# Layer 0's routed experts in two sets of sorted tokens, with the engines' orders written out; in layer 1's tail, weight loads issued by GpSimd and a flag without a memset

## The chip, the cores and the metric

The kernel runs on one core of a Trainium2 chip. A core has five engines with an instruction stream each: TensorE (PE in the profile, its weight loads PEld), VectorE (DVE), ScalarE (ACT), GpSimd (POOL) and SyncE (SP); an engine executes its stream in order and waits on semaphores for the others. DMAs are issued by SP, ACT or POOL and run on 16 DMA engines. The metric is the device time of one execution in microseconds (us), the median over runs. All arithmetic here is in float32.

## The reference

Two transformer layers with adaptive layer norm over 8 sequences of 256 tokens, width 128: 2048 tokens. Cut to what matters:

```python
mod = (_silu(L0_c) @ L0_wmod).reshape(8, 6, 1, -1)          # sa, ca, ga, sb, cb, gb per sequence
h = _layernorm(x) * (1 + ca) + sa
x = x + ga * _L0_attn_ref(h, ...)                            # 16 heads of 8, causal
h = _layernorm(x) * (1 + cb) + sb
x = x + gb * _L0_ffn_ref(h, ...)

# _L0_ffn_ref: 8 experts, hidden width 512, top 2
shared = new_gelu(xf @ Wfc_s + bfc_s) @ Wproj_s + bproj_s
probs = jax.nn.softmax(xf @ Wr, axis=-1)
topk_p, topk_i = jax.lax.top_k(probs, 2)
topk_p = topk_p / jnp.sum(topk_p, axis=-1, keepdims=True)
gate = gate.at[jnp.arange(N)[:, None], topk_i].add(topk_p)
for e in range(8):
    h = new_gelu(xf @ Wfc[e] + bfc[e]) @ Wproj[e] + bproj[e]
    routed = routed + h * gate[:, e:e + 1]

# layer 1: the same frame; 16 heads of 64, causal; its feed-forward:
router = jax.nn.sigmoid(x @ gate_w + gate_b)                 # 16 experts, width 64, top 2, normalised
all_outputs = einsum(silu(hg) * hu, experts_wd)
return x + _mlp(x, shared_wg, shared_wu, shared_wd) + expert_weighted
```

The two gates of a token in layer 0 are a softmax over the two best logits, since the rest of the softmax cancels when they are divided by their sum.

## The kernel before, in words

Tokens stay in SBUF as `x`, in 4 windows (`NW`) of 512 tokens (`TW`), each of 4 token tiles (`TT`) of 128. `h` holds the transposed, modulated layer norm of a window. Two batches (sequences) make one window. The framework's scheduler orders each engine's instructions by itself, except inside `tc.manual_schedule()`, where the order of the source is the order on every engine; before the change that covers only layer 1's tail.

*Attention of layer 0.* `pipelined` runs 24 units (8 batches, 3 units each): `scores0` computes scores, exponentials (ACT) and causal selects (POOL, line 789); `values0` multiplies by the values two units later, and at a batch's end takes the reciprocal (line 1148) and `finish0` projects (line 1161) and adds to `x`. `also0(n)` runs beside each unit: it pops one step from a list, `st0["steps"]`, into which the layer norm of the next feed-forward window (`layernorm_steps`, parts `normalise` and `modulate`) and `route0` are put when a window's two batches are done. So windows 0 to 2 are normalised and routed inside the attention, window 3 after it.

*Sorting.* `Sorted` moves the tokens of a layer's routed experts into DRAM (`xs`), sorted by expert. Each expert has a region of `cap` rows, all tokens that could come to it. `place` computes the rank of a token in its expert by a matmul of ones with the selection masks, writes row indices (`idx`, line 886), and issues eight indirect scatters for a window from POOL (line 889: 4 tiles, 2 choices). `apart` declares that the scatters of one object don't depend on each other; the last of them stands for all, and every read of `xs` waits for it. `tables`, after the last window, works out some 30 small arrays on DVE: which 128 rows each further tile reads (`rowi`), of which expert (`widx`), and the rows at which each token's two results will lie (`yidx`). An expert's first 128 tokens are a tile of their own; the rest, in tiles of 128, are at most `nd` further tiles. For 2048 tokens with 2 choices each there are 31 of them: 8 + 31 = 39 expert tiles.

*Layer 0's experts* (scheduler's order, lines 1189 to 1295). `wst` are the packed weights of the eight experts (514 KB each; five loaded early, three as the attention's buffers go, line 1194). `shared_hidden(w)` and `shared_project(w)` compute the shared expert for a window; the second also adds the routed experts' output bias by the gates (line 1217), multiplies by `gb` on DVE, and adds to `x` on POOL (line 1221). Then each of 39 tiles: `fetch` (SP load `xg`, for further tiles a POOL indirect load `wt` of an expert's weights, line 994), `turn_tile` (PE transpose, line 1249), `hidden` (4 matmuls, each of two passes, line 1259, and 4 gelus on ACT, line 1261), `project` (line 1270, copied on DVE and stored to `ys` by SP, lines 1274 and 1275). `fetch` runs three tiles ahead, with 4 buffers for `xg`, 5 for `wt`.

*Beginning of layer 1.* `gather(b)` brings the two results of each token of a batch back, with 4 indirect loads from POOL (line 1002), and `combine(b)` weighs and adds them to `x` (lines 1402 to 1406, DVE). Four gathers and `after0(0)` (two combines, then `normalise` and `modulate` of window 0: lines 732 to 753) stand ahead of `project1(0, part)` (line 1416), the first work of layer 1's attention. The other windows follow inside it through `also1`, which pops two steps per unit: gathers of batches 4 to 7, and `after0(1)`, `after0(2)`, `after0(3)`.

*Layer 1's tail* (written order). Windows 0 to 2 of the routed experts run sorted (`z1`), in 10 blocks `m` of four tiles: `turn1`, `hidden1`, `project_tiles` (lines 1587, 1597, 1611). Blocks 0 to 3 use resident weights, 4 and 5 are loaded earlier by SP; `fetch_weights1(m)` loads those of blocks 6 to 9, four transfers of 128 KB each. Here ACT reads the expert's number into a register and issues a plain DMA (line 1648). `tables(ps, rows)` writes `widx` as an expert's first row; with `rows` true it writes one row number per partition, which an indirect load needs. In between, the last window is normalised and routed step by step (`route1_steps`); it is then computed densely (`ffn1_hidden`, `ffn1_project`), while `gather1` and `combine1` bring back the results of the sorted blocks, 24 indirect loads. `flag` checks the reciprocals of all softmaxes (line 1728) for a general path that is not taken here.

Buffers: `ps_a`, `ps_b`, `ps_c` are PSUM tiles with 3, 2 and 3 buffers.

Of the kernel before, what the change touches and what calls it, by code (L numbers as in the profile page):

```python
# [9 lines left out]
F32 = mybir.dt.float32  # L10
# [3 lines left out]
ALU = mybir.AluOpType  # L14
# [19 lines left out]
WF, WB, WPK = FC * P, 2 * FC * P, 2 * FC * P + FC  # L34
R_MIN, R_MAX = 1e-30, 1e20
# [522 lines left out]
def fast_path(ctx: ExitStack, tc: tile.TileContext, i: dict, out: bass.AP, bad: bass.AP):  # L558
# [244 lines left out]
    def top2(*args):  # L803
        for step in top2_steps(*args):
            pass

    def top2_steps(pool, p, s12, best, tag):
# [7 lines left out]
        for k in range(2):  # L815
# [6 lines left out]
            if k == 0:  # L822

                nc.vector.scalar_tensor_tensor(work, s12[:, :, 0, :], -4.0, p, ALU.mult, ALU.add)
                yield
# [6 lines left out]
    class Sorted:  # L832
# [29 lines left out]
        def place(self, n, tokens, ps_):  # L862
# [24 lines left out]
            for j in range(nt):  # L887
                for k in range(2):
                    self.apart(nc.gpsimd.indirect_dma_start(  # L889
                        out=self.xs[:, :], out_offset=bass.IndirectOffsetOnAxis(ap=idx[:, j, k : k + 1], axis=0),  # L890
                        in_=tokens[:, j, :], in_offset=None,
                    ).ins)
# [122 lines left out]
    z0 = Sorted(xp, "0", E0, NW, TT, (2 * NT - 2) // P)  # L1015
    z1 = Sorted(xp, "1", E1, 3, TT, ND1)
    z0.clear(zero)
# [15 lines left out]
    def route0(w, ps_):  # L1033
# [7 lines left out]
        red = r0p.tile([P, TT, 1], F32, tag="red", bufs=2, name=f"red0_{w}")  # L1041
        nc.vector.tensor_reduce(red, lg, AX.X, ALU.max)
        nc.vector.tensor_tensor(p, lg, red.to_broadcast(shape), ALU.subtract)
        nc.scalar.activation(p, p, AF.Exp)
        nc.vector.tensor_reduce(red, p, AX.X, ALU.add)
        nc.vector.reciprocal(red, red)
        nc.vector.tensor_tensor(p, p, red.to_broadcast(shape), ALU.mult)
        s = z0.s12[:, t4]
        g = g12[:, t4]
        top2(r0p, p, s, g, f"0_{w}")  # L1050
        z0.place(w, tokens0[w], ps_)
        pick = r0p.tile([P, TT, 2, E0], F32, tag="pickg", bufs=2, name=f"pickg0_{w}")

        nc.vector.tensor_tensor(red, g[:, :, 0:1], g[:, :, 1:2], ALU.add)
        nc.vector.reciprocal(red, red)
        nc.vector.tensor_tensor(g, g, red.to_broadcast([P, TT, 2]), ALU.mult)
# [3 lines left out]
    with (  # L1060
# [108 lines left out]
        def also0(n):  # L1169
            b, u = divmod(n, 3)  # L1170
            if st0["steps"]:
                st0["steps"].pop(0)()
# [4 lines left out]
            if u == 2 and b:  # L1177
                finish0(b - 1)
                if b % 2 == 0:
                    w = b // 2 - 1  # L1180
                    st0["steps"] += layernorm_steps(w, md[0], SB, CB, f"0b{w}", ps_ln, make_tokens0)
                    st0["steps"].append(lambda w=w: route0(w, ps_ln))

        project0(0)
        pipelined([(b, u) for b in range(B) for u in range(3)], scores0, values0, 2, also0)
        finish0(B - 1)

# [3 lines left out]
    with tc.tile_pool(name="ff0", bufs=2) as fp0:  # L1191
# [31 lines left out]
        last = layernorm_steps(NW - 1, md[0], SB, CB, f"0b{NW - 1}", ps_b, make_tokens0)  # L1223
        last[0]()
        hs = shared_hidden(0)
        last[1]()
        route0(NW - 1, ps_b)
        shared_project(0, hs)

        z0.tables(ps_b, True)  # L1230

# [3 lines left out]
        def fetch(n):  # L1235
            xg = fp0.tile([P, P], F32, tag="xg", bufs=4, name=f"xg_{n}")
            if n < E0:
                nc.sync.dma_start(out=xg, in_=z0.xs[bass.ds(n * z0.cap, P), :])
                wt = wst[n]
            else:  # L1240
                z0.load_rows(xg, n - E0)
                wt = fp0.tile([P, WPK], F32, tag="wt", bufs=5, name=f"wt_{n}")
                z0.load_weights(wt, i["wpk"], n - E0)
            st["x", n] = xg, wt

        def turn_tile(n):
            xg, wt = st["x", n]
            xT_ps = ps_b([P, P], f"xT_{n}")
            nc.tensor.transpose(xT_ps, xg, ident)  # L1249
            xT = fp0.tile([P, P], F32, tag="xT", bufs=3, name=f"xTs_{n}")  # L1250
            nc.vector.tensor_copy(xT, xT_ps)
            st["xT", n] = xT

        def hidden(n):
            xT, wt = st.pop(("xT", n)), st["x", n][1]
            hp = ps_a([P, FC, P], f"hp_{n}")
            hs = fp0.tile([P, FC, P], F32, tag="hst", bufs=3, name=f"hst_{n}")
# [6 lines left out]
            st["hs", n] = hs  # L1264

        def project(n):
            hs, wt = st.pop(("hs", n)), st.pop(("x", n))[1]
            y = ps_c([P, P], f"yt_{n}")
# [4 lines left out]
            ysb = fp0.tile([P, P], F32, tag="ysb", bufs=3, name=f"ysb_{n}")  # L1273
            nc.vector.tensor_copy(ysb, y)  # L1274
            nc.sync.dma_start(out=z0.ys[bass.ts(n, P), :], in_=ysb)

        for n in range(3):
            fetch(n)
        for w in range(1, NW):
            hs = shared_hidden(w)  # L1280
            shared_project(w, hs)
        NTI = E0 + z0.nd
        turn_tile(0)
        for n in range(NTI + 1):
            if n + 3 < NTI:
                fetch(n + 3)
            if n + 1 < NTI:
                turn_tile(n + 1)
            if n < NTI:
                hidden(n)  # L1290
            if n:
                project(n - 1)
# [20 lines left out]
    def route1_steps(w, ps_):  # L1313
# [17 lines left out]
        yield from top2_steps(r1p, p, s, g, f"1_{w}")  # L1331
# [38 lines left out]
    with (  # L1370
# [16 lines left out]
        st1 = {"steps": []}  # L1387

        def gather(b):

            yg = ap1.tile([P, 2, 2, P], F32, tag="yg", bufs=2, name=f"yg_{b}")
            for j in range(2):
                z0.gather(yg[:, j], 2 * b + j)
            st1["yg", b] = yg

        def combine(b):

            yg = st1.pop(("yg", b))
            t = ap1.tile([P, 2, P], F32, tag="t", name=f"tc_{b}")
# [492 lines left out]
```

## Time and profile before

| what | value |
|---|---|
| median of 3 runs | 689.07 us (688.54 to 689.54) |
| the profiled execution | 690.99 us |
| its span in the trace | 688.7 us (2.3 us lie around it) |
| mean granted TensorE clock | 0.929 |
| PE busy | 571.4 us (83%) |
| POOL busy | 308.8 us (45%) |
| DVE busy | 331.0 us (48%) |
| ACT busy | 252.8 us (37%) |
| layer 0's attention: last output matmul ends | 150.7 us |
| first and last tile of the routed experts of layer 0 | 193.2 and 271.3 us |
| layer 1's first projection | 298.3 us |
| last gathers of layer 1 | 650.4 to 680.3 us |

All times of instructions count from the start of the span. In timeline lines the columns are: start, busy time, engine, source line, operation, output<-inputs, shape, count, and in brackets the idle time of the engine before it with what ended it. A queue of an engine (SPq, ACTq, POOLq) issues DMAs. The page also cuts the span in 40 slices with the busy share in tenths. Busy shares average over stages with different limits, so each stage has to be read by itself.

### The profile page before, as it was taken

How to read it: one execution, taken by the hardware profiler on the slowest of the kernel's cores; microseconds unless marked ns; L12 is line 12 of the kernel's file. 1: busy time of each engine (PE TensorE's matmuls, PEld its weight loads, DVE VectorE, ACT ScalarE, POOL GpSimd, SP SyncE). 2: the span in 40 equal slices, each digit the busy share in tenths (PEclk: the TensorE clock that was granted, in tenths of full speed). 3: DMA queues.
4: the chain of work that ended last, by engine and by line, in shares of the span. 5: the costliest groups of instructions: out<-in, count | busy, mean ns of one | idle time of the engine just before them, and what ended most of it. 6: DMA issues, size and time to landing. Idle time of an engine off the chain costs nothing.

```text
span 688.7 us, 12844 instructions
## 1 busy us (share of the span) xinstructions
PE 571.4 (83%) x4899; PEld 404.7 (59%) x4899; DVE 331.0 (48%) x985; ACT 252.8 (37%) x447; POOL 308.8 (45%) x458
## 2 busy tenths in 40 slices
PE   3899878878999997078999998999899958658890
PEld 3455444445799997045667765776576636546460
DVE  5367747674522222374243565254524471534573
ACT  2446343526345555014342363234323521142130
POOL 6576584854713442774121146314631462020173
PEclk9999998999999999569999999999999988977996
DMA  8999940012466995120020203020303043443722
GB/s 288 317 407 400 373 173 9 25 45 83 133 229 207 320 338 176 50 53 21 1 63 1 63 2 81 12 64 1 81 13 63 1 125 101 121 120 92 160 69 81
DMA packets 51712, 85.41 MB, mean 124 GB/s; under 512 B 6332, under 2 KB 29916, under 8 KB 50492
## 3 DMA queue, kind: packets, MB, share of 16 engines
q1 hardware_dynamic: 40940, 57.64, 26.6%
q0 software_dynamic: 8400, 24.78, 11.2%
q10 hardware_dynamic: 2304, 2.10, 1.0%
q8 instruction: 40, 0.66, 0.4%
q14 instruction: 28, 0.23, 0.1%
HBM read 53.43 MB, written 31.07 MB: 123 GB/s over the span
## 4 chain that ended last, share of the span: by engine, by line
PE 36%; DVE 6%; DMA 6%; POOL 5%; issue 3%; ACT 2%; ACTq 1%; SPq 0%; DVEq 0%; POOLq 0%
PE o L1461 5%; PE sc L1441 5%; PE y L1512 4%; PE qp L1416 4%; PE vp L1424 4%; PE kp L1416 4%; POOL yg L1002 3%; PE sum L1469 3%; DMA yg<-ys,yidx 3%; DMA rb<-rd 2%; PE gu L1597 1%; DVE r L1476 1%; POOL xs L889 1%; PE yq L1611 1%; DMA wt<-in_wpk_dram 1%
## 5 line engine op out<-in xcount | busy, mean ns | idle before, releaser
L789 POOL TENSOR_SCALAR_AFFINE_SELECT pt<-pt 128x256 f32<-128x256 f32 (+1 forms) x176 | 89.7, 540 | 152.9 <-ACT pt L1444 133.8
L1444 ACT ACTIVATE pt<-sc 128x768 f32<-128x768 f32 x64 | 48.9, 808 | 87.1 <-PE sc L1441 87.0
L1002 POOL DMA_INDIRECT yg<-ys,yidx x56 | 53.4, 953 | 56.1 <-ACT a L1679 39.6
L889 POOL DMA_INDIRECT xs<-ht,idx x56 | 60.9, 1087 | 23.9 <-issue 14.5
L1117 ACT ACTIVATE pt<-sc 128x1024 f32<-128x1024 f32 x48 | 46.8, 1021 | 53.7 <-PE sc L1113 52.7
L1461 PE MATMUL o<-pt,v 128*64 128x128 f32 (+1 forms) x512 | 53.5, 343 | 5.3 <-POOL pt L789 5.3
L1441 PE MATMUL sc<-q,k 64*128 64x256 f32 (+1 forms) x512 | 55.5, 343 | 0.0
L1441 PEld LDWEIGHTS sc<-q,k 64*128 64x128 f32 x512 | 43.6, 190 | 16.1 <-issue 11.5
L1461 PEld LDWEIGHTS o<-pt,v 128*64 128x64 f32 x512 | 34.2, 141 | 31.1 <-issue 11.4
L994 POOL DMA_INDIRECT wt<-in_wpk_dram,widx x31 | 29.2, 941 | 46.4 <-PE xT L1249 45.0
L593 DVE COPY k<-kp 128x512 f32<-128x512 f32 x29 | 20.1, 692 | 53.7 <-PE kp L1416 53.7
L1261 ACT ACTIVATE hst<-hp,wt 128x128 f32<-128x128 f32 x124 | 35.4, 368 | 26.6 <-ACT hst L1261 17.6
L1113 PE MATMUL sc<-qm,k 32*128 32x512 f32 x192 | 35.9, 681 | 5.0 <-POOL qm L1088 4.4
L1416 PE MATMUL kp<-h,wk 128*128 128x256 f32 x128 | 36.6, 412 | 1.9 <-DVE v L593 1.9
L1416 PE MATMUL qp<-h,wq 128*128 128x256 f32 x128 | 37.6, 413 | 0.6 <-DVE h L753 0.6
L1424 PE MATMUL vp<-wv,h 128*128 128x512 f32 x64 | 37.8, 675 | 0.0
L1274 DVE COPY ysb<-yt 128x128 f32<-128x128 f32 x39 | 11.4, 292 | 54.7 <-PE yt L1270 48.8
L595 ACT COPY v<-vp 128x512 f32<-128x512 f32 x29 | 17.0, 585 | 53.3 <-PE vp L1424 42.6
L593 DVE COPY ou<-o 128x512 f32<-128x512 f32 x29 | 19.9, 687 | 32.1 <-PE o L1461 32.0
L1259 PE MATMUL hp<-xTs,wt 128*128 128x128 f32 x248 | 33.5, 278 | 1.5 <-DMA wt<-in_wpk_dram,widx 0.6
L1270 PE MATMUL yt<-wt,hst 128*128 128x128 f32 x248 | 32.6, 275 | 0.0
L1512 PEld LDWEIGHTS y<-wo,ou 128*128 128x128 f32 x256 | 29.6, 194 | 3.9 <-issue 2.6
(284 smaller groups left out, 1121.4 us busy)
## 6 DMA issues: line engine op xcount, KB each, us to landing
xs<-zero SPq DMA_DIRECT2D x1, 12288.0 KB
xs<-zero SPq DMA_DIRECT2D x1, 8192.0 KB
rb<-rd SPq DMA_DIRECT2D x14, 512.0 KB
wst<-in_wpk_dram SPq DMA_DIRECT2D x8, 514.0 KB
mdb<-mrd SPq DMA_DIRECT2D x2, 2048.0 KB
xg<-xs SPq DMA_DIRECT2D x63, 64.0 KB
ys<-ysb SPq DMA_DIRECT2D x10, 256.0 KB
ys<-ysb SPq DMA_DIRECT2D x39, 64.0 KB
```

The lines of the kernel that those rows point to most:

```text
L593: nc.vector.tensor_copy(dst, src)
L789: nc.gpsimd.affine_select(out=pt, in_=pt, compare_op=ALU.is_ge, fill=0.0, base=0, pattern=[[0, pt.shape[1]], [1, P]], channel_multiplier=-1,)
L889: self.apart(nc.gpsimd.indirect_dma_start(out=self.xs[:, :], out_offset=bass.IndirectOffsetOnAxis(ap=idx[:, j, k : k + 1], axis=0), in_=to ...
L1002: nc.gpsimd.indirect_dma_start(out=yg[:, k, :], out_offset=None, in_=self.ys[:, :], in_offset=bass.IndirectOffsetOnAxis(ap=self.yidx[:, j, ...
L1113: nc.tensor.matmul(out=sc[:, n, :].rearrange("p (a q) -> p a q", q=rhs.shape[2]), lhsT=k[r, cols], rhs=rhs, start=True, stop=True,)
L1117: nc.scalar.activation(pt[:, bass.ts(half, 2), :], sc, AF.Exp)
L1416: nc.tensor.matmul(out=ps_[:, n, :], lhsT=w1[f"w{what}1"][:, bass.ts(2 * part + n, P)], rhs=hb, start=True, stop=True,)
L1424: nc.tensor.matmul(out=vp, lhsT=hb[:, bass.ts(j, P)], rhs=w1["wv1"][:, bass.ts(k, 512)], start=True, stop=True)
L1441: nc.tensor.matmul(out=sc[:, n, cols], lhsT=k[r, c % 2, bass.ts(kb, P)], rhs=q[r, c % 2, qs], start=True, stop=True)
L1444: nc.scalar.activation(pt, sc[:, :, 0:384], AF.Exp, scale=1.0 / math.sqrt(D1))
L1461: nc.tensor.matmul(out=o[bass.ts(n, D1), m, qs], lhsT=v[:, kb, bass.ts(4 * u + 2 * m + n, D1)], rhs=pts[m][:, n, cols], start=(kb == 0), s ...
L1512: nc.tensor.matmul(out=y[:, j, :], lhsT=aT[:, c % 2, c // 2, bass.ts(j, P)], rhs=w1["wo1"][:, c, :], start=(c == 0), stop=(c == NC1 - 1),)
```

## The change

*Two sets.* `z0` becomes `zs0`: one `Sorted` for windows 0 to 2 (23 further tiles, 31 in all) and one for window 3 (7 further tiles, 15 in all), with tables of their own. The tables of the first set are a step of the attention's list.

*Routing of layer 0* becomes a generator with a `yield` between steps. It drops the softmax: the two best are chosen from copied logits, and the gates come from the difference of the two, by one exponential. `also0` pops two steps per unit.

*Written order* now begins before the expert stage and ends after `project1(0, ...)`. Only window 0 of the shared expert stands ahead of the tiles; windows 1 to 3 come after them. In the loop over 46 tiles each iteration takes one step of a chain: first the rest of window 3 (layer norm, logits, choice, placing with one scatter per iteration, gates, tables), later, once the first set is done, gathers and combines of batches 0 to 3 and the layer norm of layer 1's window 0. `fetch` runs four ahead. The layer norm of layer 1's window 1 stands between the shared windows.

*Layer 1's beginning.* Gathers of batches 0 to 3 and `after0(0)`, `after0(1)` are gone from there; `also1` still gathers batches 4 to 7 and runs `after0(2)` and `after0(3)`.

*Tail.* `fetch_weights1` uses `load_weights`, indirect loads from POOL, with row tables; the flag uses a column of an existing array in place of a memset tile, and its matmul comes one step later.

```diff
-    z0 = Sorted(xp, "0", E0, NW, TT, (2 * NT - 2) // P)
+    zs0 = [Sorted(xp, f"0{n}", E0, k, TT, (2 * k * TW - 2) // P) for n, k in enumerate((NW - 1, 1))]
...
-        nc.vector.tensor_reduce(red, lg, AX.X, ALU.max)
-        nc.vector.tensor_tensor(p, lg, red.to_broadcast(shape), ALU.subtract)
-        nc.scalar.activation(p, p, AF.Exp)
-        nc.vector.tensor_reduce(red, p, AX.X, ALU.add)
-        nc.vector.reciprocal(red, red)
-        nc.vector.tensor_tensor(p, p, red.to_broadcast(shape), ALU.mult)
-        s = z0.s12[:, t4]
+        nc.vector.tensor_copy(p, lg)
+        yield
+        z, n = (zs0[0], w) if w < NW - 1 else (zs0[1], 0)
+        s = z.s12[:, bass.ts(n, TT)]
+        best = r0p.tile([P, TT, 2], F32, tag="best", bufs=2, name=f"best0_{w}")
+        yield from top2_steps(r0p, p, s, best, f"0_{w}", LOW)
+        yield
+        yield from z.place_steps(n, tokens0[w], ps_)
+        yield
...
+        nc.vector.tensor_tensor(d, best[:, :, 1:2], best[:, :, 0:1], ALU.subtract)
+        nc.scalar.activation(d, d, AF.Exp)
+        nc.vector.tensor_scalar(g[:, :, 0:1], d, 1.0, None, ALU.add)
+        nc.vector.reciprocal(g[:, :, 0:1], g[:, :, 0:1])
+        nc.vector.tensor_tensor(g[:, :, 1:2], g[:, :, 0:1], d, ALU.mult)
...
-            if st0["steps"]:
-                st0["steps"].pop(0)()
+            for step in st0["steps"][:2]:
+                step()
+            del st0["steps"][:2]
...
+                    if w == NW - 2:
+                        st0["steps"].append(lambda: zs0[0].tables(ps_ln, True))
...
+    manual = ExitStack()
+    manual.enter_context(tc.manual_schedule())
...
-        last = layernorm_steps(NW - 1, md[0], SB, CB, f"0b{NW - 1}", ps_b, make_tokens0)
-        last[0]()
-        hs = shared_hidden(0)
-        last[1]()
-        route0(NW - 1, ps_b)
-        shared_project(0, hs)
-
-        z0.tables(ps_b, True)
...
+        def last_tokens():
+
+            normalise, modulate = layernorm_steps(last, md[0], SB, CB, f"0b{last}", ps_b, make_tokens0)
+            normalise()
+            yield
+            modulate()
+            yield
+            yield from route0_steps(last, ps_b)
+            yield
+            zs0[1].tables(ps_b, True)
+
+        def first_batches():
+
+            for b in range(2):
+                gather(b, fp0)
+                yield
+                yield
+                yield
+            for b in range(2):
+                combine(b, fp0)
+                gather(b + 2, fp0)
+                yield
+                yield
+            normalise, modulate = layernorm_steps(0, md[1], SA, CA, "1a0", ps_b)
+            normalise()
+            yield
+            modulate()
+            yield
+            for b in range(2, 4):
+                combine(b, fp0)
+                yield
+
+        for n in range(4):
+            fetch(*tiles[n])
+        hs = shared_hidden(0)
+        chain = last_tokens()
+        next(chain)
+        turn_tile(*tiles[0])
+        shared_project(0, hs)
+        for n in range(len(tiles) + 1):
+            if n + 1 < len(tiles):
+                turn_tile(*tiles[n + 1])
+            if n < len(tiles):
+                hidden(*tiles[n])
+            if n:
+                project(*tiles[n - 1])
+            if n + 4 < len(tiles):
+                fetch(*tiles[n + 4])
+            if n == first + 1:
+                assert next(chain, None) is None
+                chain = first_batches()
+            if n:
+                next(chain, None)
...
+        hs = shared_hidden(1)
+        normalise, modulate = layernorm_steps(1, md[1], SA, CA, "1a1", ps_b)
         for w in range(1, NW):
-            hs = shared_hidden(w)
-            shared_project(w, hs)
...
+            done, hs = hs, shared_hidden(w + 1) if w < last else None
+            shared_project(w, done)
+            if w == 1:
+                normalise()
+        modulate()
...
-            if u == 0 and b % 2 == 0 and b + 2 < B:
-                st1["steps"] += after0(b // 2 + 1)
-
-        for b in range(4):
-            gather(b)
-        for step in after0(0):
-            step()
+            if u == 0 and b % 2 == 0 and b + 4 < B:
+                st1["steps"] += after0(b // 2 + 2)
+
         for part in range(4):
             project1(0, part)
+        manual.close()
...
-                d = 4 * m + t - E1
-                r = nc.values_load(
-                    z1.widx[0:1, d : d + 1], engines=[mybir.EngineType.Activation], min_val=0,
-                    max_val=(E1 - 1) * P, skip_runtime_bounds_check_because="an expert's number, 128 times",
-                )
-                nc.scalar.dma_start(out=wt[:, t, :], in_=i["wpk1"][bass.ds(r, P), :])
+                z1.load_weights(wt[:, t, :], i["wpk1"], 4 * m + t - E1)
...
-            ones = small.tile([P, 1], F32, tag="ones", bufs=1, name="good_ones")
-            nc.vector.memset(ones, 1.0)
+            yield
             cnt = ps_b([1, 1], "good_cnt")
-            nc.tensor.matmul(out=cnt, lhsT=whole, rhs=ones, start=True, stop=True)
+            nc.tensor.matmul(out=cnt, lhsT=whole, rhs=nums[:, 1:2], start=True, stop=True)
```

## The prediction

> **What bounds the kernel now.** I read the slices of the page first, for stages and holes; then busy times by stretches around the largest hole; then the timeline there and in the tail; then single lines for pitches.
>
> ```profile
> PE   3899878878999997078999998999899958658890
> ...
> POOL 6576584854713442774121146314631462020173
> PEclk9999998999999999569999999999999988977996
> ```
>
> PE fills nearly every slice. The holes are slice 16 (17.2 us a slice), the start, the very end, and a thinner stretch in the tail (5, 8, 6, 5, 8). Behind slice 16 the clock stands at 5 and 6 tenths.
>
> ```profile
> core 0: us, PE busy (x) PEld busy (x) DVE busy (x) ACT busy (x) POOL busy (x), PEclk, DMA share, GB/s
> ...
> 271.00:284.00 13.00, 0.28 (x3) 0.09 (x1) 2.89 (x13) 1.02 (x1) 8.78 (x9) 0.60 0.15 41
> 284.00:297.00 13.00, 0.38 (x2) 0.40 (x3) 7.22 (x29) 0.30 (x1) 9.71 (x11) 0.50 0.19 50
> 297.00:310.00 13.00, 12.36 (x37) 7.74 (x35) 10.67 (x40) 2.60 (x5) 9.95 (x11) 0.71 0.21 56
> ```
>
> For 26 us PE works 0.66 us, while POOL works 18.5. The timeline says what it waits for:
>
> ```profile
> 269.33 1.95 PE L1270 MATMUL yt<-wt,hst 128*128 128x128 f32 x16
> ...
> 274.39 0.95 POOL L1002 DMA_INDIRECT yg<-ys,yidx  x1 [0.15 <-issue]
> ...
> 278.00 0.94 POOL L1002 DMA_INDIRECT yg<-ys,yidx  x1 [0.30 <-issue]
> ...
> 296.62 1.09 PE L749 MATMUL nt1a<-ident,xn1a 128*128 128x128 f32 x4 [25.34 <-DVE xn1a L740]
> ...
> 298.34 2.08 PE L1416 MATMUL qp<-h,wq 128*128 128x256 f32 x4 [0.64 <-DVE h L753]
> ```
>
> The last expert tile ends at 271.28; GpSimd gathers one half token tile every 1.25 us (0.95 + 0.30), and layer 1's first projection waits for a window of them: 27.1 us. In the 78.1 us before (first tile 193.19) 39 tiles cost PE 2.0 each; steady state 1.9 (0.1 turn + 0.9 hidden + 0.9 project).
>
> In the tail ACT issues four plain loads per expert block; its next work stands behind them, and PE behind ACT:
>
> ```profile
> 594.21 4.03 ACTq L1648 DMA_DIRECT2D wt<-in_wpk_dram  x4
> ...
> 602.11 0.58 ACT L1589 COPY xTs<-xT 128x512 f32<-128x512 f32 x1 [2.24 <-DMA wt<-in_wpk_dram]
> ...
> 604.89 1.23 PE L1611 MATMUL yq<-wd,aq 64*128 64x128 f32 x8 [8.57 <-DVE aq L1603]
> ```
>
> **The change, part by part.** P1 below is the start of layer 1's first projection, 298.34 now.
>
> *End of layer 0's attention.* In the order of the changed program seven of window 2's eight token scatters stand on POOL between the two halves of the last batch's last causal select.
>
> ```profile
> 147.63 1.04 POOL L889 DMA_INDIRECT xs<-ht,idx  x1 [1.70 <-DVE mv0b L734]
> ...
> 150.02 0.71 PE L1161 MATMUL y<-wout,aT 128*128 128x128 f32 x4 [2.33 <-DVE aT L1150]
> ```
>
> Now the scatters run 147.63–157.6, beside and after the end of attention (150.73). Two steps per unit instead of one bring the indices some 5 us forward, to 142.5. The seven scatters (7 × 1.27 = 8.9) end at 151.4; then the select 1.1, last values about 1.1, reciprocal 1.76, product 0.43, output 0.71: 156.5, with a little for hand-overs 157. So +6.3. Bounds: +2 (indices another 4 us earlier), +10 (windows 0 and 1, whose scatters also stand before a select, pay as well).
>
> *Start of the tiles.* Three shared windows move behind the tiles; only window 0 (3.45 + 4.46 = 7.9) stays ahead. Three weight loads of 514 KB are issued as attention's buffers go (151.80 now), and the first token loads queue behind them on SP; the three landed about 6.5 later. xT of tile 0 stands in PE's order ahead of the shared projection. I take 13.0 from attention's end to the first tile: 7.9 work, 5.1 stall (bounds 1 and 7). First tile at 170, not 193.2.
>
> *Iterations 0–32.* 33 × 1.9 = 62.7. Window 3's normalise, logits and ranks, which ran ahead of the tiles, now run among them: 0.66 + 1.06 + 0.4 + 0.2 = 2.3 of PE. Its eight scatters share POOL with the weights, one each per tile: 1.27 + 1.26 = 2.5 against 1.9 of PE, for eight tiles: 5.0 late, mostly taken up by a four-tile lead (landing 5.6), 0.6 left. The gate's exponential needs a table load (1.28) and back, and some 30 small DVE operations of the tables at 0.22 (6.6) stand ahead of a tile's copy: 6.2 late. Ranks 1.0, loads 1.0. Together 62.7 + 2.3 + 8.8 = 73.8 (stalls 3 to 14).
>
> *Set 2.* Splitting 39 tiles into 31 and 15 adds seven, 7 × 1.9 = 13.3. On POOL sixteen gathers for the first batches now stand between the seven weight loads of this set: gather(0) at iteration 32, then 35, 38 and 40, the last load behind all of them.
>
> ```profile
> L994 POOL DMA_INDIRECT wt<-in_wpk_dram,widx x31: 936/936/1002, 181.8 to 262.7; - x31
> ...
> DMA to landing us min/median/max: 5.0/5.6/5.9
> ```
>
> (16 + 7) × 1.25 = 28.75; from 0.3 after iteration 32 the last issue starts at 27.8 and lands at 32.9 (5.1, near the least of the row, since DMA is calmer without the stream of loads); then one hidden 0.9, project 0.9 and the gelu between: end at 36.0. PE alone would need 14 × 1.9 = 26.5. Stall 9.5; bounds 2 (0.94 a piece, back to back: 23 × 0.31 = 7.1 less) and 13 (landing 5.9, landing waits of gathers of about 2.5). The Trainium skill ("DMA: Bandwidth & Descriptors", Anatomy of one DMA — SWDGE (gpsimd) path) fits a load as 2.0 us and bytes at 436 GB/s, an estimated 3.2 for these 526 KB. The row says 5.0 to 5.9 and decides; by the page the stall would be 7.6, the median 693.
>
> *Behind the tiles.* Three shared windows: 3 × 7.9 = 23.7 plus a transpose 1.0 of PE, and 3.6 for a normalise that must wait for POOL's add (1.27), square root and gelu tables (1.28 each): 28.3. The 27.1 us hole is gone, because gathers and normalise of the first window lie under tiles and shared windows.
>
> *Sum to P1.* 157.0 + 13.0 + 73.8 + 36.0 + 28.3 = 308.1, against 298.3: +9.8. Without any stall (0 for 5.1, 8.8, 9.5, 3.6 and the 6.3) it would be 274.8: −23.5, the far end.
>
> *Layer 1's beginning.* Gathers for batches 4–7 start 2.9 before P1 now (295.48); afterwards they stand behind the addition and a memset of layer 1, 2.3 after it, and DVE's evacuations stand behind their combines. Value evacuation of batch 1 ended 24.3 after P1 (321.98 + 0.69); I take 27.4: +3.1 (bounds 0 and 6).
>
> *Tail weights.* ACT loses 16 plain loads and register reads; POOL gains 16 indirect loads × 1.25 = 20 us from 594 on, where it shows only four additions of 1.27 up to 611. The last issue is out at about 617, its block needs it at 626, so I count no stall on them. ACT's square root (598.27, 7.5 behind the loads) and the copy go forward: yq 604.89 by 5.0. The second block (613.77–616.88, two loads either side of an exponential) gives 1.4, the third (copy 627.40) 0.3, and the half-clock stretch of 619–630 some 0.5. Together −7.2; bounds −8.6 and 0 (a rotated buffer or a late landing holds ACT's successors anyway). What it costs if cover is gone: the 20 us of POOL. The end is set by 24 gathers × 1.25 from 650.42, behind the results' landing, so what comes earlier counts fully. The same page (SWDGE vs HWDGE vs iDMA) gives plain transfers to SP or ACT and irregular ones to GpSimd, against this move. The trace shows ACT held for 8 us by plain loads, and no run yet shows the alternative; by the rule the 7.2 would be nothing, the median 702.
>
> *Flag.* One memset less (about 0.1) and the matmul a step later. PE's wait there (2.16 at 648.25) lies beside the wait for gathers: 0. If that cover were gone it could cost 2. The softmax left out of layer 0's routing saves some DVE operations of 0.22, in the slack of the attention; nothing. The clear of layer 0's sorted tokens (8192 KB) goes in two parts of the same bytes, early, under attention: nothing, and its time on SP if it were late.
>
> *Total.* 9.8 + 3.1 − 7.2 = +5.7 on the span: 694.4; the profiled execution has 690.99, so 696.7, and 1.92 above the median before, so a median of 694.8, rounded to 695.0.
>
> **The rivals.** *GpSimd keeps up in set 2* (faster). The stall of 9.5 falls towards 2 if pieces follow at 0.94 instead of 1.25. For it: 0.94 is their own busy time, and PE needs no gather itself. Against: 0.30 is "issue" between nearly all indirect DMAs of the trace, whichever they are. From 0.93 a piece (7.3 saved) it passes 687.7; with it attention's end, which hangs on the same pitch (7 × 0.31 = 2.2 less): 695.0 − 7.1 − 2.2 = 685.7. Chance 0.25, and in it the cases where several stalls are smaller than I take them.
>
> *The tail gives nothing.* POOL's loads come late or ACT still waits where it did: 695.0 + 7.2 = 702.2. For it: the loads take a buffer that an earlier block frees (594.21 follows the yq of 594.00), whoever issues them. Against: POOL idles 29 us before 601.38. Decides from 7 us of lateness in the first block. Chance 0.17.
>
> *Nothing nets out.* The gain of the hole and tail equals the seven tiles and stalls: 689 ± 1.4; chance 0.08. That the change doesn't do what it says could hold only for the attention, where the scheduler still orders; from the tiles on the order is written out.
>
> **How the numbers follow.** Forecast 0.50, own range 690.5 to 700: stall bounds of about ±5 around 695. Faster 0.25, even 0.08, worse 0.17. For 8 in 10 I leave about a tenth below and above: 682 (the faster rival with the start's stall at 1) to 705 (tail nothing and 3 more at attention's end). A measurement of this kernel tells 0.2%, 1.4 us, from no change: faster 0.25, same 0.08, slower 0.50 + 0.17 = 0.67.
>
> **What would show it.** In the profile after: PE idle before the last values of attention 0 with a POOL select as releaser (about 5); the first tile near 170; hidden matmuls of the last seven tiles released by weight DMAs, 9.5 in sum, with POOL busy without holes from tile 32 on; the first projection of layer 1 near 308; the tail without ACT loads, the yq after normalise 5 nearer to the block before it, and the first of the last gathers 7 nearer to layer 1's end of attention. I am wrong if P1 is below 298, or if set 2's hidden matmuls wait for nothing.

## The result and the profile after

The changed kernel takes 723.88 us (median of 4 runs, 722.22 to 731.64) against 689.31 us for the kernel before on the same chip: ratio 1.0497, 95% interval 1.0389 to 1.0604. The profiled execution took 724.94 us with a span of 723.2 us, 34.5 us more than before. The forecast was 695.0 us with a range of 682 to 705: the direction was right, the size was not. The experiments below were run in five groups, each with the kernel before beside it; in the first, the third and the fifth, called disturbed here, the kernel before itself took 722 to 725 us instead of 689 to 694, and every trace kept from them has idle times put down to a releaser "remote" (47 to 109 us summed over the engines), which no trace of the others has, so their numbers are set beside the kernel before of the same group and nothing else.

The same rows of the page's slices (18.1 us each), now of the changed kernel:

```profile
PE   3898787767786888788799999899989986878990
...
POOL 6665667550364317404712123541562156073174
PEclk9999898977999999999899999999999997978996
```

The hole of slice 16 is gone: no slice between the expert stage and the last one is empty, and none there has a clock below 7 tenths. But slices 3 to 15 hold 6, 7 and 8, where the kernel before has 9 in half of them. One deep hole became many shallow ones. The busy times by stage show how many (from the end of attention; the last stretch is the three shared windows):

```profile
core 0: us, PE busy (x) PEld busy (x) DVE busy (x) ACT busy (x) POOL busy (x), PEclk, DMA share, GB/s
164.00:181.00 17.00, 13.57 (x56) 9.47 (x56) 3.57 (x16) 6.79 (x8) 0.00 (x0) 0.72 0.32 112
181.00:200.00 19.00, 15.31 (x122) 14.66 (x122) 7.78 (x32) 7.12 (x25) 7.84 (x12) 0.91 0.31 91
200.00:235.00 35.00, 26.36 (x198) 25.21 (x198) 11.72 (x60) 16.23 (x51) 17.90 (x19) 0.90 0.74 223
235.00:271.00 36.00, 30.04 (x253) 28.21 (x252) 7.77 (x28) 16.54 (x59) 9.07 (x10) 1.00 0.70 201
271.00:308.00 37.00, 29.14 (x236) 27.83 (x235) 16.34 (x62) 18.26 (x58) 21.75 (x23) 0.95 0.57 171
308.00:337.00 29.00, 24.82 (x151) 18.35 (x149) 7.58 (x26) 10.89 (x15) 3.27 (x3) 1.00 0.04 11
```

In the second, third and fourth stretch (iterations 0 to 32) PE idles 18.3 of 90 us, and part of what it does runs at a lowered clock (0.91, 0.90). The waits of PE over the tile loop name the releaser (us in total, times, longest):

```profile
PE xT L1280 <- DMA xg<-xs: 15.5, 15, 2.4
PE hp L1290 <- DMA wt<-in_wpk_dram,widx: 6.6, 3, 2.9
PE hp L1290 <- DVE xTs L1282: 2.6, 2, 2.4
PE rk L879 <- POOL pre L875: 0.8, 1, 0.8
PE rk L878 <- DVE m L870: 0.5, 1, 0.5
```

The largest line is one that the forecast counted at 1 us: the loads of a tile's 128 sorted rows. In the tile loop of the kernel before, the same line reads:

```profile
PE xT L1249 <- DMA xg<-xs: 0.6, 1, 0.6
```

| stage (us of the span; length from the event before) | before | forecast | after |
|---|---|---|---|
| end of layer 0's attention | 150.7 | 157.0 | 164.8 |
| first tile | 193.2 | +13.0 | 180.9 (+16.1) |
| end of iteration 32 | – | +73.8 | 271.2 (+90.3) |
| last tile ends | 271.3 | +36.0 | 307.8 (+36.6) |
| layer 1's first projection (P1) | 298.3 | +28.3, so 308.1 | 337.2 (+29.4) |
| P1 to the tail's first transpose | 283.7 | +3.1 | 284.4 (+0.7) |
| tail's first transpose to the end | 106.7 | −7.2 | 101.6 (−5.1) |

38.9 + 0.7 − 5.1 = 34.5. The timeline shows how a row load comes late. In the kernel before (start, duration, then the instruction), SP issues a tile's load 0.3 us after the transpose that frees its buffer, and only then the store of results:

```profile
217.81 0.27 PE L1249 MATMUL xT<-ident,xg 128*128 128x128 f32 x1
218.11 0.33 SPq L990 DMA_DIRECT2D xg<-xs  x1
218.54 0.39 SPq L1275 DMA_DIRECT2D ys<-ysb  x1
```

That load is for the tile four further, 7.6 us later at 1.9 a tile. In the changed kernel the store stands ahead of the load:

```profile
211.92 0.27 PE L1280 MATMUL xT<-ident,xg 128*128 128x128 f32 x1
...
212.44 0.33 SPq L1306 DMA_DIRECT2D ys<-ysb  x1
...
213.32 0.34 SPq L992 DMA_DIRECT2D xg<-xs  x1
...
217.95 0.33 PE L1280 MATMUL xT<-ident,xg 128*128 128x128 f32 x1 [1.43 <-DMA xg<-xs]
```

The load at 213.32 is tile 14's and the transpose at 217.95 uses it: 4.63 us from issue to use, of which PE waited 1.43. The store of tile 9's results (212.44) has to wait for tile 9's projection and its copy, so the load of tile 14 leaves SP 6.9 us after the transpose that freed its buffer (tile 10's, at 206.44). For each load that PE waits for, the lead is shorter than the landing. Whether the landing itself has become slower as well, no trace shows; in the loop before, PE waited for one such load only (0.6 us, the line above).

The end of attention, with the last scatters of window 2 and the select behind them on POOL:

```profile
147.17 1.05 POOL L891 DMA_INDIRECT xs<-ht,idx  x1 [1.11 <-DVE idx L887]
...
155.44 0.97 POOL L891 DMA_INDIRECT xs<-ht,idx  x1 [0.30 <-issue]
156.43 1.10 POOL L790 TENSOR_SCALAR_AFFINE_SELECT pt<-pt 128x1024 f32<-128x1024 f32 x1
...
157.58 1.71 PE L1148 MATMUL o<-pt,vm 128*32 128x128 f32 x26 [4.78 <-POOL pt L790]
...
163.62 1.20 PE L1171 MATMUL y<-wout,aT 128*128 128x128 f32 x4 [2.41 <-DVE aT L1160]
```

This is the mechanism of the forecast, seven scatters ahead of a select, with a wait of 4.78 us. The indices, however, came at 146.9 and not at 142.5.

### The profile page after: what moved, and what is told of

The parts are those of the page before. It is cut to its first block, busy times and chain, and to the rows that moved or that the text cites. A ratio compares the mean times of both kernels' runs of the same rounds, so it can differ in the third digit from the quotient of the medians.

```text
span 723.2 us, 13150 instructions
## 1 busy us (share of the span) xinstructions
PE 599.1 (83%) x5019; PEld 425.9 (59%) x5019; DVE 330.6 (46%) x1014; ACT 266.6 (37%) x479; POOL 325.7 (45%) x475
## 5 line engine op out<-in xcount | busy, mean ns | idle before, releaser
L790 POOL TENSOR_SCALAR_AFFINE_SELECT pt<-pt 128x256 f32<-128x256 f32 (+1 forms) x176 | 90.3, 542 | 141.3 <-ACT pt L1505 128.6
L996 POOL DMA_INDIRECT wt<-in_wpk_dram,widx x46 | 43.8, 952 | 56.7 <-PE yq L1669 22.6
L1502 PEld LDWEIGHTS sc<-q,k 64*128 64x128 f32 x512 | 43.5, 191 | 15.5 <-issue 11.4
L1305 DVE COPY ysb<-yt 128x128 f32<-128x128 f32 x46 | 13.4, 291 | 64.5 <-PE yt L1301 64.5
L1148 PE MATMUL o<-pt,vm 128*32 128x128 f32 (+1 forms) x512 | 33.8, 364 | 7.3 <-POOL pt L790 7.3
L1290 PEld LDWEIGHTS hp<-xTs,wt 128*128 128x128 f32 x240 | 31.5, 205 | 10.2 <-DVE xTs L1282 5.2
```

What stands on the lines that cost most here:

```text
L790: nc.gpsimd.affine_select(out=pt, in_=pt, compare_op=ALU.is_ge, fill=0.0, base=0, pattern=[[0, pt.shape[1]], [1, P]], channel_multiplier=-1,)
L996: nc.gpsimd.indirect_dma_start(out=wt, out_offset=None, in_=packed, in_offset=bass.IndirectOffsetOnAxis(ap=self.widx[:, d : d + 1], axis=0),)
L1290: nc.tensor.matmul(out=hp[:, c, :], lhsT=wt[:, bass.ts(c, P)], rhs=xT, start=True, stop=True)
L1502: nc.tensor.matmul(out=sc[:, n, cols], lhsT=k[r, c % 2, bass.ts(kb, P)], rhs=q[r, c % 2, qs], start=True, stop=True)
```

## The experiments

**The row loads on SP (theory A).** In the changed kernel the load of the rows is issued right after the transpose that frees its buffer, which puts it two result stores earlier in SP's order; the weights' load stays.

```diff
                 turn_tile(*tiles[n + 1])
+            if n + 5 < len(tiles):
+                fetch_rows(*tiles[n + 5])
...
             if n + 4 < len(tiles):
-                fetch(*tiles[n + 4])
+                fetch_weights(*tiles[n + 4])
```

> The changed kernel with one move: each tile's row load (xg) is issued on SP right after the transpose that frees its buffer, ahead of the store of an earlier tile's results, as in the kernel before; weights stay where they are. Theory A (the written order put the row load on SP behind that store, which cut its lead from four tiles to about 2.4 us): the 15.5 us that PE waits for xg in the tile loop go, with the half clock behind them, the loop falls from 126.9 to about 109 us, total 705 to 708. Theory B (GpSimd's queue bounds the loop, as predicted): the wait moves to the weights, total 718 to 723.

Measured: 758.32 us against 724.46 before, ratio 1.0469 (1.0383 to 1.0556), in a disturbed group without the changed kernel beside it: nothing follows from it. Again, beside it:

> The changed kernel itself, as the yardstick for the kernels beside it on the same chip. All theories: 1.05 times the kernel before.

Measured: 727.08 us, before 693.65, ratio 1.0511 (1.0462 to 1.0560): the yardstick.

> The row loads ahead of the result stores on SP, again, beside the changed kernel. Theory A (SP's order cut the lead of the row loads): 15 to 19 us below the changed kernel. Theory B (the weights behind the gathers on GpSimd bound the loop): at most 5 us below it.

Measured: 711.87 us, ratio 1.0256 (1.0206 to 1.0307): 15.2 us below the changed kernel. The waits of PE in its tile loop:

```profile
PE hp L1295 <- DMA wt<-in_wpk_dram,widx: 8.8, 5, 3.1
PE hp L1295 <- DVE xTs L1287: 4.5, 3, 3.5
```

The line of xg has vanished (15.5 in the changed kernel), and the loop took 179.5 to 290.2, 110.7 us instead of 126.9 (125.1 in the changed kernel's execution of this group). Theory A holds, though the lead was not the 2.4 us of the expectation but 4.63 in the lines above. What is left at the top is the weights, 8.8, close to the forecast's 9.5 for set 2.

**The weights of set 2 (theory B, the forecast's own).** Five of the seven loads are issued ahead of the first gathers, into buffers that are free by then.

```diff
+            if first - 4 <= n <= first:
+                fetch_weights(zs0[1], E0 + n - first + 4)
             if n + 4 < len(tiles):
...
+                if n + 4 not in range(first + E0, first + E0 + 5):
+                    fetch_weights(*tiles[n + 4])
```

> The changed kernel with five of the second set's seven weight loads issued ahead of the first gathers on GpSimd, in buffers that are free by then. Theory B (GpSimd's queue in set 2): the 6.6 us of waits for weights and the half clock behind them go, total 713 to 716. Theory A (SP's order): row loads still arrive late, only part comes back, total 717 to 720; no change above 722 would say that POOL's queue is hidden.

Measured, with the row loads as in the changed kernel: 759.12 us against 724.46, ratio 1.0489 (1.0392 to 1.0587), in the same disturbed group: nothing follows from it. Together with the early row loads:

> The changed kernel with the row loads ahead of the result stores, and five of the second set's seven weight loads issued ahead of the first gathers. The forecast's term for GpSimd's queue in set 2 (9.5 us) says 7 to 10 us below the kernel with the row loads alone (ratio to the kernel before about 1.013). Rival (once the rows arrive, the later gathers and combines take the place of the weights as the wait): within 3 us of it (1.022 to 1.026).

Measured: 747.42 us against 722.61, ratio 1.0313 (1.0269 to 1.0356), above the expected value, in a disturbed group. Again:

> Row loads early and five weight loads of set 2 ahead of the first gathers, again. GpSimd's queue in set 2 as the second cause in the loop: ratio to the kernel before 1.011 to 1.017 (the row loads alone gave 1.026). Rival (combines and gathers take its place): 1.022 or more.

Measured: 702.83 us against 693.15, ratio 1.0158 (1.0064 to 1.0252), where the row loads alone gave 1.0256 in another group: about 7 us less by the ratios, whose intervals overlap. Waits of PE in its loop:

```profile
PE hp L1295 <- DVE xTs L1287: 5.9, 4, 3.6
PE hp L1295 <- DMA wt<-in_wpk_dram,widx: 3.6, 3, 2.1
```

The weights fell from 8.8 to 3.6 us, and P1 came at 316.5 instead of 321.0. So GpSimd's queue in set 2 was a real cause, but the traces show 4.5 us of it in the loop, about half of what was forecast. They differ by another 4.3 us in layer 1's tail (97.2 instead of 101.5), where this move changes nothing; that the ratio falls into the expected range is in part luck.

**The scatters ahead of the selects (theory C).** One step per unit in layer 0's attention, as before; the steps left over run after it.

```diff
-            for step in st0["steps"][:2]:
-                step()
-            del st0["steps"][:2]
+            if st0["steps"]:
+                st0["steps"].pop(0)()
...
         finish0(B - 1)
+        for step in st0["steps"]:
+            step()
```

> The changed kernel with one step per unit in layer 0's attention, as before, and the steps left over run after it. Theory C (scatters of windows 0 to 2 stand ahead of causal selects and hold PE, 4.8 us at the end of attention and again earlier, each with half clock behind it): attention ends near 151 to 153 instead of 164.8, total 711 to 714. Rival: the scatters and tables only move behind the attention, where the first tile waits for them: first tile no earlier than 178, total 719 to 724.

Measured: 757.46 us against 724.46, ratio 1.0464 (1.0382 to 1.0546), in the disturbed group of the row loads: nothing follows from it. Again, beside the changed kernel:

> One step per unit in layer 0's attention, again, beside the changed kernel. Theory C (scatters ahead of the causal selects hold PE): attention ends 11 to 14 us earlier than in the changed kernel, and the total is 10 to 13 us lower. Rival (scatters and tables move behind the attention and hold the first tile): the total within 4 us of the changed kernel.

Measured: two runs at 708 and 712 us, two at 720; their median, 715.84 us, is 11.2 us below the changed kernel, the two lower runs 15 to 19, and the ratio of 1.0242 (1.0192 to 1.0291) is that of the two lower ones. So there is a gain, but its size stays open. The trace is of an execution at 720. In it the attention ends at 152.4 instead of 162.8, and the first tile starts at 172.8 instead of 178.2: half of the gain is given back there, where PE waits 6.8 us for the first row load, which SP holds back for 8.5 us until the last scatters have landed. At P1 5.6 us are left (328.4 instead of 334.0).

The shorter attention is what theory C asked for, but not by the cause that it names. PE's waits for selects behind the scatters are 7.5 us here (3.46 at 93.00 and 3.99 at 128.20), against 7.1 in the changed kernel of the same group: the one at the end has gone, the earlier ones have grown. What fell are PE's other waits in the attention, for layer norm, routing and output (from 18.0 us to 10.0 between 54 us and the attention's end). So the two steps per unit cost the time, and the scatters are one part of it; an experiment that moves the scatters alone is missing.

**Do the causes add up?** Row loads, weights, one step per unit, and window 0's shared projection ahead of the first transpose:

```diff
         chain = last_tokens()
+        shared_project(0, hs)
         next(chain)
         turn_tile(*tiles[0])
-        shared_project(0, hs)
```

> The changed kernel with four moves together: row loads early, weights of set 2 early, one step per unit in layer 0's attention, and window 0's shared projection ahead of the first tile's transpose and the layer norm of window 3. If the causes are separate, 15 + 7 + 11 + 1 us below the changed kernel: ratio to the kernel before about 1.0 (0.995 to 1.008). If they hide one another: 1.015 or more.

Measured: 742.05 us against 722.61, ratio 1.0265 (1.0239 to 1.0291), between its two cases, in a disturbed group.

> The four moves together, again. Separate causes: ratio 0.995 to 1.008. Causes that hide one another: 1.015 or more.

Measured: 695.82 us against 693.15, ratio 1.0026 (0.9981 to 1.0070): within the first case. Attention 152.0, first tile 167.9, last tile 279.5, P1 308.8. Four changes of place take back 4.8 of the 5.1% that the changed kernel lost in the second group, with the seven tiles and the new tail still there. P1 has moved by 25.2 us (from 334.0), and the steps one by one gave 13.0, 4.5 and 5.6 without the shared projection: by these traces, of two groups, the causes are nearly separate.

**Does the idea pay without its stalls?** Further, `tables` in six pieces, one an iteration, window 0's multiplication after the first transpose, and window 1's layer norm in layer 1's attention.

```diff
+        table = zs0[0].tables_steps(ps_b, True)
         chain = last_tokens()
+        shared = shared_project_steps(0, hs)
+        next(shared)
         next(chain)
         turn_tile(*tiles[0])
-        shared_project(0, hs)
+        next(shared, None)
+        next(table)
...
+            if n < 2:
+                next(table)
             if n:
                 next(chain, None)
...
+        st1["steps"] += layernorm_steps(1, md[1], SA, CA, "1a1", ps_ln)
```

> As four_moves, and further: the tables of both sets cut into pieces between tiles and off the attention's end, window 0's result multiplied after the first transpose, and the layer norm of layer 1's window 1 moved back into layer 1's attention. Seven more tiles cost 13.3 us, the hole of 27 us is filled, the tail gives 5 to 6: if no stall of the loop is left, ratio 0.975 to 0.985, under the kernel before; if stalls of DVE and GpSimd in the loop remain, 0.99 to 1.01.

Measured: 734.47 us against 722.61, ratio 1.0159 (1.0135 to 1.0184): above both cases, in a disturbed group.

> Four moves, tables in pieces, and the layer norm of window 1 in layer 1's attention, again. If the stalls of the loop were the whole loss and two sets pay once they are gone: ratio 0.975 to 0.985, below the new tail alone on the old expert stage (0.992). If VectorE's share in the loop keeps it: 0.99 to 1.01.

Measured: 689.67 us against 693.15, ratio 0.9972 (0.9930 to 1.0014): level with the kernel before, and not below the new tail alone. P1 is at 299.8 (298.3 before): the stage with two sets is now as long as the old one with its hole. PE's waits in its loop, and behind P1:

```profile
PE hp L1306 <- DMA wt<-in_wpk_dram,widx: 6.9, 3, 3.4
PE xT L1296 <- DMA xg<-xs: 3.2, 1, 3.2
PE hp L1306 <- DVE xTs L1298: 2.3, 4, 0.7
```

```profile
PE kp L1504 <- DVE h L754: 5.5, 1, 5.5
```

The last comes from the layer norm that this version moved. To take it and the weights away: six weight buffers, six loads of set 2 ahead of the gathers, the layer norm taken after the second of the shared projections behind the tiles and only its modulation in layer 1; the shared expert's result also has one buffer instead of two.

```diff
-                wt = fp0.tile([P, WPK], F32, tag="wt", bufs=5, name=f"wt{z.tag}_{n}")
+                wt = fp0.tile([P, WPK], F32, tag="wt", bufs=6, name=f"wt{z.tag}_{n}")
...
+            if n == first:
+                fetch_weights(zs0[1], E0 + 5)
+            if n == first + E0 + 1:
+                fetch_weights(zs0[1], E0 + 6)
...
-            if w == 1:
+            if w == 2:
                 normalise()
```

> As all_moves, with six buffers for the experts' weights (six of set 2's seven loads ahead of the first gathers), window 1's layer norm taken after the second shared projection, and only its transposes and modulation in layer 1's attention. The wait of 5.5 us on that layer norm and most of 6.9 us on weights seen in all_moves_2 should go: 8 to 11 us less, ratio 0.980 to 0.988, below the new tail alone (0.993). If other waits take their place: 0.990 to 0.997.

Measured: 737.96 us against 723.32, ratio 1.0270 (1.0186 to 1.0354), outside both cases. In its trace neither of the two waits is among the large ones any more, but it fell in a disturbed group, and the largest waits of PE between 100 and 340 us are others (10.6 us for attention outputs, 9.0 for copied transposes): whether two sets can pay stays open.

**The tail alone.** The kernel before with `load_weights` for blocks 6 to 9, the row tables that it needs, and the flag's edit.

```diff
-                            lambda: z1.tables(ps_ln, False), lambda: [fetch_rows1(m) for m in range(4)],
+                            lambda: z1.tables(ps_ln, True), lambda: [fetch_rows1(m) for m in range(4)],
...
-                nc.scalar.dma_start(out=wt[:, t, :], in_=i["wpk1"][bass.ds(r, P), :])
+                z1.load_weights(wt[:, t, :], i["wpk1"], 4 * m + t - E1)
```

> The kernel before with the tail's two edits alone (weights of the last four blocks by GpSimd, flag without memset). The forecast's term says 7.2 us less, 682; the two traces, from the last projection of layer 1 to the end, say 5.1 less, 684. Rival (the loads take as long whoever issues them): 689.

Measured: 727.18 us against 724.46, ratio 1.0040 (1.0001 to 1.0079), in a disturbed group.

> The kernel before with the two edits of the tail alone, again. The term of the forecast: 7.2 us below the kernel before; the two traces: 5.1 below; rival (the loads take as long whoever issues them): no difference.

Measured: 687.22 us against 693.65, ratio 0.9927 (0.9879 to 0.9976). PE's waits in the tail, first of the kernel before, then of this one:

```profile
PE yq L1611 <- DVE aq L1603: 15.8, 7, 8.6
```

```profile
PE yq L1611 <- DVE aq L1603: 8.7, 7, 3.4
```

```profile
595.62 0.98 POOL L994 DMA_INDIRECT wt<-in_wpk_dram,widx  x1 [22.49 <-PE yq L1611]
...
600.37 0.72 PE L1611 MATMUL yq<-wd,aq 64*128 64x128 f32 x8 [3.40 <-DVE aq L1603]
```

POOL had been idle for 22.5 us when it issued the first load, and the projection that waited 8.6 waits 3.4.

> The kernel before with the new tail alone, beside the kernel of all moves, which has the new tail too. Ratio 0.990 to 0.994; what lies between it and the kernel of all moves is what the two sets and the written order are worth when their stalls are moved away.

Measured: 686.92 us against 693.15, ratio 0.9935 (0.9896 to 0.9974).

> The kernel before with the new tail alone, as the yardstick beside it: 0.990 to 0.994.

Measured: 725.01 us against 723.32, ratio 1.0085 (1.0037 to 1.0134). So the tail gives 0.7% in both groups where the kernel before runs near 693, and loses 0.4 and 0.9% in the two where it runs near 724.

**The flag alone**, on the kernel before:

> The kernel before with the flag's edit alone. The forecast says nothing (the end is set by the gathers beside it): ratio 1.000; rival: the wait of 2.2 us on TensorE goes from the end, 0.997.

Measured: 722.87 us against 722.61, ratio 1.0013 (0.9985 to 1.0040): nothing, as forecast, but in a disturbed group, where the whole tail gave nothing either. How much of the tail's 0.7% is the flag's, no run shows.

The version to keep is the kernel before with the new tail. It is below both kernels in two groups; in the two disturbed ones it isn't, and what differs there the traces don't say. Every variant that was run in both kinds of group has a ratio 0.011 to 0.024 higher in the disturbed ones, and their order is the same.

## Why the prediction was right or wrong

*End of attention: right in kind, mis-sized.* "156.5, with a little for hand-overs 157" became 164.8. The step "two steps per unit … bring the indices some 5 us forward, to 142.5" failed: they came at 146.9. Window 2 is routed after batch 5's output, and that stood at 129.41 instead of 125.05; counted from there, the two steps saved the 5 us. The delay is already there at batch 2's output (77.44 instead of 70.06), ahead of the first scatter, and PE waits there for routing work on DVE:

```profile
74.38 0.18 PE L878 MATMUL rk<-m,before 128*128 128x32 bf16 x1 [2.02 <-DVE m L870]
...
77.44 1.22 PE L1171 MATMUL y<-wout,aT 128*128 128x128 f32 x4
...
78.01 1.13 POOL L891 DMA_INDIRECT xs<-ht,idx  x1 [1.16 <-DVE idx L887]
```

For that the forecast had no term. What was only a bound ("windows 0 and 1 … pay as well") happened with 2.5 us (1.54 at 89.19 and 0.95 at 125.15). And behind the wait of 4.78 the last value matmuls took 3.6 us, at a granted clock of 0.50, where I had 1.1 for them.

*Start of the tiles.* 16.1 instead of 13.0, so 8.2 over the 7.9 of work, outside the bounds of 1 to 7. Only 3.4 of it are waits; the rest is the same work at a mean granted clock of 0.73.

*Iterations 0 to 32: here the forecast broke.* 90.3 us instead of 73.8. The step was "mostly taken up by a four-tile lead (landing 5.6)" and, for the row loads, "loads 1.0". I took the lead from the program, `fetch(n + 4)`, and compared it with the landing. A lead is what lies between the issue on its queue and the use; the queue is SP's, and there the store of tile n − 1's results, which waits for PE and DVE, stands ahead of the load. In these iterations PE waited 14.4 us for rows, where the sum had 1.0; its other waits were 3.7 instead of 7.8; and 7.2 us are left, nearly all of it time in which PE was busy for longer than its work. `rows_early_2` showed the cause: the wait of 15.5 vanished, 15.2 us came back.

*Set 2: right in the total, and in part by luck.* 36.6 instead of 36.0. The pitch of 1.25 held over gathers and loads, and the last load left 28.0 us after iteration 32 (forecast 27.8). But PE's waits for weights there were 6.6 us and not 9.5; matmuls slower than counted made up for it, and `rows_weights_2` took 4.5 us away at P1 by five loads. The rival that needed a pitch of 0.93 is refuted. The Trainium skill's fit ("DMA: Bandwidth & Descriptors", Anatomy of one DMA — SWDGE (gpsimd) path), an estimated 3.2 us for a weight load, stays below what the loop needed: the last load was issued at 299.15 and used at 303.50, 4.35 us later, after a wait of PE for it.

*Behind the tiles: right*, 29.4 for 28.3. *Layer 1's beginning*: +0.7 for +3.1, inside its bounds.

*Tail: right in kind, and too large.* −5.1 in the changed kernel (−2.9 in its execution of the second group), −6.4 and −6.1 in the spans of the new tail alone, for −7.2. The rule that gives plain loads to SP or ACT (same page, SWDGE vs HWDGE vs iDMA) would have left it out; here POOL was idle and ACT was not, and the measurement decides. *Flag*: nothing, measured in a disturbed group only.

*Stalls were converted at par.* PE's listed waits in the loop are 26.0 us. The loop has 126.9 − 89.7 (46 tiles at 1.9, and 2.3 of moved work) = 37.2 us over its work. The 11.2 us between are time in which PE is busy: 100.9 us for 89.7 of work. The mean granted clock of 0.95 makes about half of it (100.9 × 0.05 = 5.0); the rest isn't placed. The forecast had no term for either.

*Rivals.* The faster one did not occur. "The tail gives nothing" is excluded for the undisturbed groups. P1 came 29.1 us later than forecast: 16.5 in iterations 0 to 32, 7.8 in the attention, 3.1 at the start of the tiles, 1.7 behind. The largest part is there because one queue was not followed, and no rival stood on that queue.

## What to carry to other kernels

When an order is written out by hand, list for every load the instructions ahead of it on its own queue, and what each of them waits for: the lead is counted from there, not from the loop index. A store that waits for this iteration's result, put ahead of a load for a later one, takes away the prefetch. And filling a hole of 27 us with work that costs 13 us more (seven tiles) leaves some 14 us, which 46 iterations use up at 0.3 us each.

## What the runs showed of the hardware that had not been expected

A short pause is enough for half rate, and not every one does it: behind a wait of 2.42 us (at 193.43 in the changed kernel) the next sixteen matmuls took 1.68 + 1.91 us instead of 1.06 + 1.06, with a granted clock of 0.50 from 194 to 197; behind one of 2.04 (at 226.38) they took 1.06 + 1.06, at a granted clock of 1.00. The Trainium skill ("TensorE: Matmul & The Clock Gate", Part 1: The HAM clock gate) has the clock fall after at least one idle window of about 3.4 us, and calls the window free-running; here 2.4 us of idle time did it.
